# Cross-attention and soft mixture of experts on one core: second group's keys made early, norm factors folded, exponentials with sums

## The chip, the cores and the metric

The kernel runs on one core of a Trainium2 chip, in 32-bit floats throughout. The metric is device time in microseconds (us). The core has TensorE (PE), VectorE (DVE), ScalarE (ACT), GpSimd (POOL) and SyncE (SP), each with its own instruction queue that it works through in order; SP issues most of the DMAs.

## What is computed

For each of 16 batches, 100 tokens of width 256 attend to 361 context rows with 16 heads of width 16. The result goes through a soft mixture of 16 experts with 64 slots each.

```python
x = x + xattn(layernorm(x), ctx, ctx, mask, wq, bq, ..., wo, bo)   # 16 heads of 16
y = layernorm(layernorm(x)) * norm_g + norm_b
se = (layernorm(slot_embeds) * slot_g + slot_b) * scale            # 16 experts x 64 slots
logits = einsum("bnd,esd->bnes", y, se)
dispatch = softmax(logits, over the tokens n)
combine = softmax(logits, over all slots e, s)
slots = einsum("bnd,bnes->besd", y, dispatch)
h = gelu(slots @ Wg + bg) * (slots @ Wu + bu)                      # 256 -> 512
eout = h @ Wd + bd                                                 # 512 -> 256
out = x + einsum("bns,bso->bno", combine, eout)
```

## The kernel before

**Groups and stages.** The batches are worked in five groups of 2, 2, 4, 4 and 4 (line 47). For each group the attention makes the tokens' new x, then the dispatch of its logits fills slots, then 16 experts run over all slots of the group, and then the weighted sum goes to the output. The experts' weights are read again for each group, by SP's queue, into five buffers (`load_weights`, line 949).

**Attention.** `query_work` (403) normalises two batches' x, transposes it and makes queries. `key_work` (467) loads and transposes one batch's context and makes keys `kT` and values `vpad`; a row of the mask is put into `kT` by DMA (523). Keys of a batch take one of the two "kl" buffers, which the combine logits `lex` use too, so `keys_fit` (697) lets a group's keys begin only when few are held and, once one is held, when the dispatch of the groups before is done. A batch is then four units (`Unit`, 618): scores (634), maxima on VectorE (639), a transpose of the maxima (647) and their addition to the queries (649), scores again, transposed (657), exponentials on ScalarE (665), the product with the values (678). The sums come out of the same product as a further row. `out_work` (553) divides by them after the fourth unit, in two halves of 200 columns (565 to 568), multiplies with `wo`, adds x and normalises twice over in one step (597). POOL, or VectorE in the first group, multiplies by `norm_g` and adds `norm_b` (600, 601).

**Dispatch.** `slot_work` (362) makes the normalised slot embeddings `seT` once. `dispatch_quarter` (762) does four experts of two batches: logits `lg` (777); maxima over the tokens on VectorE (787) and a copy to `lgs` on ScalarE (789), both from the same PSUM tile; subtraction on POOL (794), exponentials (808), sums and reciprocal on VectorE (819, 820), product on POOL (822); transposes of these weights, `d_t` (829), and the slots `sl` (839), which VectorE (850) and ScalarE (853) write to the ring. `lgs` is transposed too, `lex_t` (805), for the softmax over slots in `combine_weights` (860).

**Experts.** `experts` (1001) makes for each expert gate `gp` and up `up` (1020), gelu on ScalarE (1031), the product `hT` on VectorE (1036), and in `down` (969) the product `dn` (981). `combine_quarter` (910) adds up the outputs.

**The ring.** One SBUF tile of 10240 columns holds slots and expert outputs, a region for each quarter of a group (740). Group 0 uses columns 0 to 4095. At the start the first columns hold slot embeddings and mask.

**What sets the order.** The order on each engine is fixed when the kernel is built. Every piece of work is a generator (`Task`, 95) that yields the time at which its next step can run and how many PSUM banks it needs. The loop at line 1080 keeps a planned clock for each engine (`Clock`, 55), with a cost for each operation, and picks the first task that is ready; units and dispatch come before side work (`fill`), experts last. Four PSUM banks of one tag, `mm`, are shared by all products but the scores. While the experts have not begun and nothing is ready on PE, the loop puts in a product of the identity with itself, `warm` (1068, 1118). These fillers give PE something to do and are not used.

```python
            if not begun and now + 0.2 < ready[first] and ck.bank_ready(1) <= now and now > 8.0:
                warm_up()
                continue
```

Of the kernel before, what the change touches and what calls it, by code (L numbers as in the profile page):

```python
# [115 lines left out]
def xattn_ffn_kernel(  # L116
# [101 lines left out]
    NPAR = 4 + E * FC  # L218
    par1 = const.tile([NPAR, P], F32, name="par1")
    par2 = const.tile([E * FC, P], F32, name="par2")  # L220
    for i, v in enumerate((slot_g, slot_b)):
        nc.gpsimd.dma_start(par1[2 * i : 2 * i + 2, :], v.rearrange("(a p) -> a p", p=P))
    nc.gpsimd.dma_start(par1[4:NPAR, :], bg.rearrange("e (a p) -> (e a) p", p=P))
# [26 lines left out]
    vpads = []  # L250
    for i in range(2):
        vp = const.tile([P, 3, H * 32], F32, name=f"vpad{i}")
        vp = vp.rearrange("p c (x k w) -> p c x k w", k=4, w=HD)
        for c in range(3):
            nc.vector.memset(vp[:, c, :, 1:3, :], 0.0)
            nc.vector.memset(vp[:, c, :, 1:3, 0:1], 1.0)
        vpads.append(vp)
# [21 lines left out]
    sb_c = [sgb[:, i : i + 1] for i in (2, 3)]  # L279

# [31 lines left out]
    def parameter_work():  # L312
# [5 lines left out]
        load_bc("ng", norm_g)  # L318
        load_bc("nb", norm_b)
        for _ in range(3):  # L320
            load_weights(0)
        yield 22.0, 1
# [38 lines left out]

    def slot_work():
# [3 lines left out]
        for c in range(ES // P):  # L366
            yield (lambda: max(25.0, ck.t["DVE"])), 0
            t = ck.run("DVE", stats(se[:, c, :], P, mv[:, c, :]))
# [7 lines left out]
        for c in range(ES // P):  # L376
            yield (lambda: max(t, ck.t["ACT"])), 0
# [19 lines left out]
        seT_t[0] = last  # L397

    seT_t = [NEVER]
    with_bo = {}  # L400
    qps, keys, values_t, cxs_of, out_t = {}, {}, {}, {}, {}
# [65 lines left out]
    def key_work(b):  # L467
# [20 lines left out]
        kT = None  # L488
        for oc in range(KD):
            yield (lambda: max(t, par_t[0], 7.0) if kT or keys_fit(b) else NEVER), 1  # L490
            if not kT:
                live.add(b)
                kT = two.tile([P, KD, 2, S2], F32, tag="kl", name="kT")
# [34 lines left out]
        vp = vpads[b % 2]  # L528
# [24 lines left out]
    def out_work(b):  # L553
# [3 lines left out]
        cxs, t = cxs_of[b]  # L557
        comb = cxs[:, 0]
        yield t, 0
        rs = const.tile([P, 2, KD, N], F32, tag="rs", name="rs")  # L560
        t2 = t
        for par in range(2):
            if par:
                yield t, 0
            nc.vector.stream_shuffle(rs[:, par], cxs[:, par], [MAXROW[par]] * 32)
            nc.vector.reciprocal(rs[:, par], rs[:, par])
            t = ck.run("DVE", 1.65, t)
            nc.gpsimd.tensor_tensor(cxs[:, par], cxs[:, par], rs[:, par], ALU.mult)
            t2 = ck.run("POOL", 0.6, t)
        yield t2, 0  # L570
        nc.vector.tensor_tensor(comb, comb, cxs[:, 1], ALU.add)
        t = ck.run("DVE", 0.3, t2)
# [26 lines left out]
        engine = nc.gpsimd if g else nc.vector  # L599
        engine.tensor_tensor(z, z, bcs["ng"][:N], ALU.mult)  # L600
        engine.tensor_tensor(z, z, bcs["nb"][:N], ALU.add)
        t = ck.run("POOL" if g else "DVE", 1.45 if g else 0.7, t)
# [15 lines left out]
    class Unit:  # L618
# [11 lines left out]
        def maxima(self):  # L630
# [11 lines left out]
            self.t = ck.run("DVE", 1.66, ck.run("PE", 0.7, self.q_t, self.k_t, free_t[0]))  # L642
# [9 lines left out]
        def exponentials(self):  # L652
# [13 lines left out]
            self.t = free_t[0] = ck.act("exp", 1200, ck.run("PE", 0.7, self.t))  # L666
            if self.cb == 3:
                live.remove(self.b)

        def values(self):  # L670
            if self.cb == 0:
                live_cxs.add(self.b)
                cxs_of[self.b] = [two.tile([P, 2, KD, N], F32, tag="cxs", name="cxs"), 0.0]
            cx = mm_tile("cx")
            for c in range(3):
                n = KC if c < 2 else S2 - 2 * KC
                for r in range(4):
                    nc.tensor.matmul(  # L678
                        cx[32 * r : 32 * r + 32, :N],
                        lhsT=vpads[self.b % 2][  # L680
# [6 lines left out]
            nc.scalar.copy(cxs_of[self.b][0][:, self.par, self.oc, :], cx[:, :N])  # L687
            t = ck.copy(100, ck.run("PE", 0.55, self.t, values_t[self.b], ck.bank()))
            ck.free(t)
            cxs_of[self.b][1] = t  # L690

    free_t = [0.0]
    group_of = {b: g for g, n in enumerate(GROUPS) for b in range(starts[g], starts[g] + n)}
# [14 lines left out]
    def units(g):  # L708
        last = None

        def finish(u):
            u.values()
            if u.cb == 3:
                fill.append(Task(out_work(u.b), ck))
                if u.b + 1 in group and u.b + 2 in group:
                    fill.append(Task(key_work(u.b + 2), ck))
# [45 lines left out]
    def dispatch_quarter(g, p, q):  # L762
# [3 lines left out]
        def gate():  # L766
# [4 lines left out]
            return max(seT_t[0], out_t[starts[g] + b0 + 1])  # L771
# [13 lines left out]
        lgv = lg[:, : 4 * N].rearrange("p (c n) -> p c n", n=N)  # L785
        mx = two.tile([P, 4], F32, tag="mx", name="d_mx")
        nc.vector.tensor_reduce(mx, lgv, AX.X, ALU.max)  # L787
        lgs = two.tile([P, 4, N], F32, tag="lgs", name="lgs")
        nc.scalar.copy(lgs, lgv)  # L789
        tl = ck.copy(400, t)  # L790
        t = ck.psum_dve(400, t)
        ck.free(max(t, tl))
        ex = two.tile([P, 4, N], F32, tag="ex", name="d_ex")
        nc.gpsimd.tensor_tensor(ex, lgs, mx.unsqueeze(2).to_broadcast([P, 4, N]), ALU.subtract)  # L794
        t = ck.run("POOL", 0.95, t, tl)
        yield (lambda: max(t - 0.3, tl) if (g, p) in live or len(live) < 2 else NEVER), 1
# [11 lines left out]
        nc.scalar.activation(ex, ex, AF.Exp)  # L808
        t = ck.act("exp", 400, t)
# [7 lines left out]
        yield t, 0  # L817
        sm = two.tile([P, 4], F32, tag="sm", name="d_sm")
        nc.vector.tensor_reduce(sm, ex, AX.X, ALU.add)
        nc.vector.reciprocal(sm, sm)  # L820
        t = ck.run("DVE", 0.75, t)
        nc.gpsimd.tensor_tensor(ex, ex, sm.unsqueeze(2).to_broadcast([P, 4, N]), ALU.mult)
# [365 lines left out]
```

## Time and profile before

| | us |
|---|---|
| median of 3 runs | 1240.83 (1240.37 to 1244.67) |
| the profiled execution | 1242.1 |
| its span, first to last instruction | 1240.1 |
| mean granted TensorE clock | 0.994 of full |
| first expert product starts | 114.28 |
| PE without work until 20 us / 20 to 78 / 78 to 106 | 7.9 / 0.33 / 0.43 |

A line of a profile's timeline reads: start, duration, engine, source line, operation, output <- inputs, shapes, how many records; in brackets the idle time of the engine before it and what ended that. A 32-bit product is two records, a transpose one. "PEld" is the load of PE's stationary operand, which runs beside the products. A wait that names an engine is inferred from semaphores: it ended last there.

### The profile page before, as it was taken

Reading aid. Unit: us, or ns where it says so; the run is one execution under the profiler, and the core shown is the slowest. Engines: PE = TensorE matmul, PEld = TensorE weight load, DVE = VectorE, ACT = ScalarE, POOL = GpSimd, SP = SyncE. Lnnn points to the kernel's source line nnn. Section 1 sums busy time; section 2 is a strip of 40 time slices with the busy share of each in tenths; the row PEclk is TensorE's granted clock in tenths of the full one; section 3 lists DMA queues with packets and bytes.
Section 4 is the critical chain, followed back from the end, with each engine's and each line's share of the span. In section 5 each row is a group of like instructions: output and inputs, shape, how many; then the busy total and the mean of one; then the engine's idle time right before and its main releaser. Section 6 shows DMA issues by size and latency. Waiting matters only on the chain.

```text
span 1240.1 us, 23091 instructions
## 1 busy us (share of the span) xinstructions
PE 1213.2 (98%) x9545; PEld 1004.7 (81%) x9545; DVE 572.5 (46%) x1193; ACT 482.6 (39%) x844; POOL 126.8 (10%) x174
## 2 busy tenths in 40 slices
PE   7999999999999999999999999999999999999998
PEld 5887888887888887778777777878888888888887
DVE  4555654566455467644535446545322245322222
ACT  2425354554444454544453436434111164311111
POOL 2111010021011112101101001211000011000000
PEclk9999999999999999999999999999999999999999
DMA  7000577621766631144333321133454432445542
GB/s 215 23 15 2 160 205 215 201 89 53 221 215 199 204 105 38 33 137 122 98 115 103 111 74 40 58 114 119 128 160 154 128 94 86 132 145 156 159 140 78
DMA packets 109329, 150.11 MB, mean 121 GB/s; under 512 B 6257, under 2 KB 67881, under 8 KB 109225
## 3 DMA queue, kind: packets, MB, share of 16 engines
q1 hardware_dynamic: 108336, 146.84, 39.1%
q8 instruction: 76, 1.25, 0.4%
q0 software_dynamic: 608, 1.53, 0.4%
q10 hardware_dynamic: 280, 0.26, 0.1%
q14 instruction: 29, 0.23, 0.1%
HBM read 146.95 MB, written 1.66 MB: 120 GB/s over the span
## 4 chain that ended last, share of the span: by engine, by line
PE 91%; DVE 3%; DMA 3%; ACT 2%; issue 1%; SPq 0%; DVEq 0%; ACTq 0%
PE gp L1020 18%; PE dn L981 18%; PE up L1020 18%; PE po L919 5%; PE sl L839 4%; PE at L657 4%; PE at L634 4%; PE lg L777 4%; PE cx L678 3%; PE warm L1071 3%; PE k_ps L496 2%; PE v_ps L534 2%; PE o_ps L576 1%; PE c_t L886 1%; PE d_t L829 1%; PE lex_t L805 1%
## 5 line engine op out<-in xcount | busy, mean ns | idle before, releaser
L1020 PE MATMUL gp<-ring,wg 128*128 128x256 f32 (+1 forms) x1280 | 247.3, 340 | 0.9 <-DMA wg<-in_L_ffn_Wg_dram 0.9
L1020 PE MATMUL up<-ring,wu 128*128 128x256 f32 (+1 forms) x1280 | 246.1, 339 | 1.5 <-DMA wu<-in_L_ffn_Wu_dram 1.5
L1036 DVE SCALAR_TENSOR_TENSOR hT<-up,parT,ge 128x256 f32<-128x256 f32 (+1 forms) x320 | 120.0, 425 | 276.0 <-PE up L1020 197.0
L1031 ACT ACTIVATE ge<-gp,parT 128x256 f32<-128x256 f32 (+1 forms) x320 | 117.0, 429 | 323.0 <-PE gp L1020 312.6
L981 PE MATMUL dn<-wd,hT 128*128 128x256 f32 x1024 | 235.4, 380 | 0.0
L1020 PEld LDWEIGHTS gp<-ring,wg 128*128 128x128 f32 x1280 | 203.6, 191 | 26.1 <-issue 5.3
L1020 PEld LDWEIGHTS up<-ring,wu 128*128 128x128 f32 x1280 | 204.4, 191 | 23.4 <-DMA wu<-in_L_ffn_Wu_dram 1.7
L981 PEld LDWEIGHTS dn<-wd,hT 128*128 128x128 f32 x1024 | 190.7, 190 | 26.1 <-DVE d_mx L787 0.5
L639 DVE TENSOR_REDUCE mxp<-at 100x4 f32<-100x1444 f32 x64 | 106.2, 1660 | 52.2 <-PE at L634 51.9
L991 DVE TENSOR_TENSOR ring<-dn,bd_bc 128x512 f32<-128x512 f32 (+1 forms) x80 | 46.7, 584 | 132.8 <-PE dn L981 132.8
L665 ACT ACTIVATE aT<-at 121x1200 f32<-121x1200 f32 x64 | 75.0, 1171 | 55.7 <-PE at L657 41.5
L1031 ACT ACT_TABLE_LOAD x51 | 65.4, 1283 | 46.6 <-PE gp L1020 38.6
L839 PE MATMUL sl<-disp,xn 100*128 100x256 f32 x256 | 64.0, 394 | 5.2 <-DVE vpad L541 4.9
L665 ACT ACT_TABLE_LOAD x43 | 55.2, 1283 | 35.4 <-DVE q L649 20.9
L919 PE MATMUL po<-ring,combT 64*100 64x256 f32 x512 | 60.7, 383 | 0.0
L839 PEld LDWEIGHTS sl<-disp,xn 100*128 100x128 f32 x256 | 48.0, 194 | 14.8 <-DVE vpad L541 6.1
L634 PE MATMUL at<-kT,qp 32*100 32x361 f32 x512 | 55.7, 504 | 2.9 <-DMA kT<-mrow_d 2.9
L657 PEld LDWEIGHTS at<-q,kT 32*121 32x121 f32 x1536 | 46.4, 180 | 15.0 <-issue 9.9
L678 PEld LDWEIGHTS cx<-aT,vpad 120*32 120x32 f32 (+1 forms) x1536 | 32.2, 110 | 32.5 <-issue 23.9
L657 PE MATMUL at<-q,kT 32*121 32x100 f32 x1536 | 57.1, 277 | 0.0
L794 POOL TENSOR_TENSOR d_ex<-lgs,d_mx 128x400 f32<-128x400 f32 x32 | 27.3, 853 | 286.3 <-ACT lgs L789 284.0
L919 PEld LDWEIGHTS po<-ring,combT 64*100 64x100 f32 x512 | 41.7, 163 | 15.3 <-issue 4.9
(124 smaller groups left out, 1207.1 us busy)
## 6 DMA issues: line engine op xcount, KB each, us to landing
wg<-in_L_ffn_Wg_dram SPq DMA_DIRECT2D x80, 512.0 KB
wu<-in_L_ffn_Wu_dram SPq DMA_DIRECT2D x80, 512.0 KB
wd<-in_L_ffn_Wd_dram SPq DMA_DIRECT2D x80, 512.0 KB
bd_bc<-in_L_ffn_bd_dram SPq DMA_DIRECT2D x80, 128.0 KB
c_sb<-in_ctx_dram SPq DMA_DIRECT2D x16, 240.0 KB
c_sb<-in_ctx_dram SPq DMA_DIRECT2D x16, 121.0 KB
acc<-in_x_dram SPq DMA_DIRECT2D x8, 200.0 KB
out_dram<-acc SPq DMA_DIRECT2D x8, 200.0 KB
```

The lines of the kernel that those rows point to most:

```text
L634: nc.tensor.matmul(self.at[:N, r, :S2], lhsT=self.q[rows], rhs=self.k[rows], start=True, stop=True)
L639: nc.vector.tensor_reduce(mxv[:, :, m : m + 1], self.at[:N, :, :S2], AX.X, ALU.max, negate=True)
L657: nc.tensor.matmul(self.at[: KC + 1, r, c * N : (c + 1) * N], lhsT=self.k[rows, c * KC : c * KC + KC + 1], rhs=self.q2[rows], start=True, ...
L665: nc.scalar.activation(self.aT[: KC + 1], self.at[: KC + 1, :, : 3 * N], AF.Exp)
L678: nc.tensor.matmul(cx[32 * r : 32 * r + 32, :N], lhsT=vpads[self.b % 2][:n, c, 4 * self.oc + r, 2 * self.par : 2 * self.par + 2, :].rearra ...
L777: nc.tensor.matmul(lg[:, c * 2 * N : (c + 1) * 2 * N], lhsT=seT[:, kd, (2 * q + c) * P : (2 * q + c + 1) * P], rhs=xnTs[g][:, kd, b0 * N : ...
L839: nc.tensor.matmul(sl[:, kd * 256 : (kd + 1) * 256], lhsT=xns[g][:, b0 + i, kd * P : (kd + 1) * P], rhs=disp[:, i, :], start=True, stop=True,)
L919: nc.tensor.matmul(pos[i][:N, :D], lhsT=combs[g, p, q][rows, j, :], rhs=eouts_of(g, q)[rows, j, p, :], start=j == 0, stop=j == QE - 1,)
L981: nc.tensor.matmul(dn[:, i * D : (i + 1) * D], lhsT=hts[fc // FB][0].rearrange("p (f t) -> p f t", f=FB)[:, fc % FB, tt * P : (tt + 1) * P ...
L1020: nc.tensor.matmul(ps[:, f * T : (f + 1) * T], lhsT=weights[k][kind][:, kd, fc * P : (fc + 1) * P], rhs=slots_of(g, q)[:, j, kd].rearrange ...
L1031: nc.scalar.activation(ge[:, cols], ps[:, cols], AF.Gelu, bias=col(4, e, fc))
L1036: nc.vector.scalar_tensor_tensor(out=hT[:, cols], in0=ps[:, cols], scalar=col(NPAR, e, fc), in1=ge[:, cols], op0=ALU.add, op1=ALU.mult,)
```

## The change

- **Keys and values early.** Keys, values and value pads of batches 2 and 3 (group 1) get places of their own in the ring, behind group 0's regions. Group 1's x, queries and keys are made while group 0's units run, without `keys_fit`. Twelve clears prepare the new value pads.
- **Division per unit.** `out_work` starts with a batch's first unit and divides after each, in four pieces of 100 columns.
- **Norm folded.** `norm_g` and `norm_b` no longer touch the tokens. `seT` is multiplied by `norm_g` (on ScalarE), `norm_b` times `seT` becomes a column `cb` added to the logits, by 16 products of one column, and both are applied to the slots when they leave PSUM.
- **Exponentials with sums.** The subtraction on POOL and the sum on VectorE go; four exponentials of 100 columns take the maxima as bias and give sums. In group 0 they read the logits in PSUM, and VectorE makes `lgs`; in later groups ScalarE makes `lgs` first and the rest reads that. In group 0 the dispatch's product with the reciprocal is on VectorE.
- **Planner.** Planned PE costs of a unit's three products are raised (0.7, 0.7 and 0.55 to 0.87, 0.85 and 0.72). Before the experts begin, side work is held back while VectorE or ScalarE has a backlog. The reciprocal of the combine sums is put later.

```diff
-    NPAR = 4 + E * FC
+    NPAR = 8 + E * FC
...
-    for i, v in enumerate((slot_g, slot_b)):
+    for i, v in enumerate((slot_g, slot_b, norm_g, norm_b)):
...
+    early_kT, early_vpads = [], []
+    def early_work():
+        at = QE * NQ * GROUPS[0] * P
+        for i in range(2):
+            yield 16.0, 0
+            early_vpads.append(value_pads(ring[:, at : at + 3 * H * 32]))
+            ck.run("DVE", 1.1)
+            at += 3 * H * 32
+            n = KD * 2 * S2
+            early_kT.append(ring[:, at : at + n].rearrange("p (k t s) -> p k t s", k=KD, t=2))
+            at += n
...
-        load_bc("ng", norm_g)
-        load_bc("nb", norm_b)
+        yield 22.0, 1
         for _ in range(3):
             load_weights(0)
-        yield 22.0, 1
...
-        seT_t[0] = last
-    seT_t = [NEVER]
+        yield last, 1
+        ps = mm_tile("cb_ps")
+        for c in range(ES // P):
+            for kd in range(KD):
+                nc.tensor.matmul(
+                    ps[:, c : c + 1],
+                    lhsT=seT[:, kd, c * P : (c + 1) * P],
+                    rhs=nb_c[kd],
+                    start=kd == 0,
+                    stop=kd == KD - 1,
+                )
+        t = ck.run("PE", 3.5, last, ck.bank())
+        nc.vector.tensor_copy(cb, ps[:, : ES // P])
+        t = ck.run("DVE", 0.15, t)
+        ck.free(t)
+        for g in range(2):
+            for kd in range(KD):
+                yield t, 0
+                dst = seT[:, kd, g * 512 : (g + 1) * 512]
+                nc.scalar.activation(dst, dst, AF.Copy, scale=ng_c[kd])
+                last = ck.copy(512, t)
+            seT_t[g] = last
+    seT_t = [NEVER, NEVER]
...
+        early = group_of[b] == 1
+        kT = early_kT[b % 2] if early else None
         for oc in range(KD):
-            yield (lambda: max(t, par_t[0], 7.0) if kT or keys_fit(b) else NEVER), 1
-            if not kT:
+            yield (lambda: max(t, par_t[0], 7.0) if kT is not None or keys_fit(b) else NEVER), 1
+            if kT is None:
...
+        vp = values_of[b] = (early_vpads if early else vpads)[b % 2]
...
+        comb = None
+        for cb in range(4):
+            yield (lambda: cx_t.get((b, cb), NEVER)), 0
+            cxs = cxs_of[b]
+            oc, par = divmod(cb, 2)
+            mine, comb = cxs[:, par, oc], cxs[:, 0]
+            rs = const.tile([P, N], F32, tag="rs", name="rs", bufs=2)
+            nc.vector.stream_shuffle(rs, mine, [MAXROW[par]] * 32)
+            nc.vector.reciprocal(rs, rs)
+            t = ck.run("DVE", 1.05, cx_t[b, cb])
+            soon = b == GROUPS[0] - 1 and cb == 3
+            (nc.vector if soon else nc.gpsimd).tensor_tensor(mine, mine, rs, ALU.mult)
+            t = ck.run("DVE", 0.25) if soon else ck.run("POOL", 0.45, t)
             if par:
                 yield t, 0
-            nc.vector.stream_shuffle(rs[:, par], cxs[:, par], [MAXROW[par]] * 32)
-            nc.vector.reciprocal(rs[:, par], rs[:, par])
-            t = ck.run("DVE", 1.65, t)
-            nc.gpsimd.tensor_tensor(cxs[:, par], cxs[:, par], rs[:, par], ALU.mult)
-            t2 = ck.run("POOL", 0.6, t)
-        yield t2, 0
-        nc.vector.tensor_tensor(comb, comb, cxs[:, 1], ALU.add)
-        t = ck.run("DVE", 0.3, t2)
+                nc.vector.tensor_tensor(comb[:, oc], comb[:, oc], mine, ALU.add)
+                t = ck.run("DVE", 0.25, t)
...
-        engine = nc.gpsimd if g else nc.vector
-        engine.tensor_tensor(z, z, bcs["ng"][:N], ALU.mult)
-        engine.tensor_tensor(z, z, bcs["nb"][:N], ALU.add)
-        t = ck.run("POOL" if g else "DVE", 1.45 if g else 0.7, t)
...
-            self.t = ck.run("DVE", 1.66, ck.run("PE", 0.7, self.q_t, self.k_t, free_t[0]))
+            self.t = ck.run("DVE", 1.66, ck.run("PE", 0.87, self.q_t, self.k_t, free_t[0]))
...
-            return max(seT_t[0], out_t[starts[g] + b0 + 1])
+            return max(seT_t[q // 2], out_t[starts[g] + b0 + 1])
...
+        def copies(t):
+            for c in range(2):
+                part = slice(2 * c, 2 * c + 2)
+                nc.scalar.activation(
+                    lgs[:, part], lgv[:, part], AF.Identity, bias=cb[:, 2 * q + c : 2 * q + c + 1]
+                )
+                t = ck.copy(200, t)
+            return t
+        def maxima(src, t):
+            nc.vector.tensor_reduce(mx, src, AX.X, ALU.max, negate=True)
+            return ck.run("DVE", 0.6, t)
+        def exponentials(src, t):
+            for i in range(4):
+                nc.scalar.activation(
+                    ex[:, i],
+                    src[:, i],
+                    AF.Exp,
+                    bias=mx[:, i : i + 1],
+                    accum_out=sm[:, i : i + 1],
+                )
+                t = ck.act("exp", 130, t)
+            return t
+        if g:
+            tl = copies(t)
+            ck.free(tl)
+            t = maxima(lgs, tl)
+        else:
+            t = exponentials(lgv, maxima(lgv, t))
+            for c in range(2):
+                part = slice(2 * c, 2 * c + 2)
+                nc.vector.tensor_scalar_add(
+                    lgs[:, part], lgv[:, part], cb[:, 2 * q + c : 2 * q + c + 1]
+                )
+                tl = ck.psum_dve(200)
+            ck.free(max(t, tl))
+        yield t, 0
+        if g:
+            t = exponentials(lgs, t)
+            yield t, 0
...
+        nc.vector.reciprocal(sm, sm)
+        t = ck.run("DVE", 0.18, t)
+        late = nc.gpsimd if g else nc.vector
+        late.tensor_tensor(ex, ex, sm.unsqueeze(2).to_broadcast([P, 4, N]), ALU.mult)
+        t = ck.run("POOL", 0.95, t) if g else ck.run("DVE", 0.6)
...
+                for kd in range(KD):
+                    nc.tensor.matmul(
+                        sl[:, kd * 256 : (kd + 1) * 256],
+                        lhsT=xns[g][:, b0 + i, kd * P : (kd + 1) * P],
+                        rhs=disp[:, i, :],
+                        start=True,
+                        stop=True,
+                    )
+                t2 = ck.pe(512, td, ck.bank())
+                for kd in range(KD):
+                    dst = slots_of(g, q)[:, :, kd, b0 + i, :]
+                    srcv = sl[:, kd * 256 : (kd + 1) * 256].rearrange("p (e s) -> p e s", s=S)
+                    if i == 0:
+                        nc.vector.tensor_scalar(dst, srcv, ng_c[kd], nb_c[kd], ALU.mult, ALU.add)
+                        t2 = ck.psum_dve(256, t2)
+                    else:
+                        nc.scalar.activation(
+                            dst, srcv, AF.Identity, bias=nb_c[kd], scale=ng_c[kd]
+                        )
+                        t2 = ck.copy(256, t2)
...
+        if not g:
+            yield t, 1
+            yield from dispatch()
...
-        nc.scalar.activation(ex, ex, AF.Exp)
-        t = ck.act("exp", 400, t)
...
-        nc.vector.tensor_reduce(sm, ex, AX.X, ALU.add)
-        nc.vector.reciprocal(sm, sm)
-        t = ck.run("DVE", 0.75, t)
-        nc.gpsimd.tensor_tensor(ex, ex, sm.unsqueeze(2).to_broadcast([P, 4, N]), ALU.mult)
-        t = ck.run("POOL", 0.95, t)
...
-        nc.vector.reciprocal(sm, sm)
-        ck.run("DVE", 0.15, t2[-1])
         for q in range(NQ):
             yield t2[-1], 1
+            if q == 0:
+                nc.vector.reciprocal(sm, sm)
+                ck.run("DVE", 0.15, t2[-1])
...
-                if group:
+                if group > 1:
                     fill.append(Task(query_work(b0), ck))
                     fill.append(Task(key_work(b0), ck))
-                fill.append(Task(key_work(b0 + 1), ck))
-                if group == 0:
+                    fill.append(Task(key_work(b0 + 1), ck))
+                elif group == 0:
+                    fill.append(Task(key_work(1), ck))
                     fill.append(Task(parameter_work(), ck))
+                    fill.append(Task(early_work(), ck))
                     fill.append(Task(slot_work(), ck))
+                    load_x(1)
+                    fill.append(Task(query_work(2), ck))
+                    fill.append(Task(key_work(2), ck))
+                    fill.append(Task(key_work(3), ck))
...
+        if not begun:
+            urgent = ("units", "out_work", "dispatch_quarter") if group < 2 else ("out_work", "dispatch_quarter")
+            soonest = min((r for t, r in zip(tasks, ready) if t.kind in urgent), default=NEVER)
+            backlog = max(ck.t["DVE"], ck.t["ACT"]) - now
+            for i, t in enumerate(tasks):
+                if t.kind in urgent or group == 0:
+                    continue
+                ready[i] = max(ready[i], now + backlog - (1.8 if t.banks else 0.6))
+                slack = {"units": 1.6}.get(t.kind, 0.6)
+                if group > 1 and now < soonest < now + slack:
+                    ready[i] = max(ready[i], soonest + 0.01)
```

## The prediction

> **What bounds the kernel now.** I read the page first (engines, then the chain), then the timeline of the first units, of the first dispatch, and the busy time by stage.
>
> ```profile
> PE 1213.2 (98%) x9545; PEld 1004.7 (81%) x9545; DVE 572.5 (46%) x1193; ACT 482.6 (39%) x844; POOL 126.8 (10%) x174
> PE 91%; DVE 3%; DMA 3%; ACT 2%; issue 1%; SPq 0%; DVEq 0%; ACTq 0%
> L1071 PE MATMUL warm<-ident 128*128 128x128 f32 x274 | 38.4, 288 | 0.0
> ```
>
> PE works from end to end and is 91% of the chain, so the time is the sum of three things: the matmuls, the gaps between them, and the filler products (`warm`) that stand where PE would wait before the first expert. A wait on another engine counts only where PE has nothing queued in front of it. The table of matmuls in the built programs is the same before and after but for the filler, 137 products before and 114 after, and 16 tiny ones. So the sum can only move through filler, those 16, and PE's idle time. Its idle time now is 26.9 us: 8.7 before 106 us (nearly all first loads), 13.8 after it, 4.4 at the end.
>
> The next view is the timeline of one unit of the first group (start, duration, engine, line):
>
> ```profile
> 39.17 1.66 DVE L639 TENSOR_REDUCE mxp<-at 100x4 f32<-100x1444 f32 x1 [1.71 <-PE at L634]
> 39.69 1.60 PE L1071 MATMUL warm<-ident 128*128 128x128 f32 x12
> 41.13 0.25 PE L647 MATMUL at<-ident,mxp 100*128 100x100 f32 x1
> 41.42 0.26 DVE L649 TENSOR_TENSOR q<-at,qp 128x100 f32<-128x100 f32 x1
> 42.00 0.89 PE L657 MATMUL at<-q,kT 32*121 32x100 f32 x24
> 42.83 1.83 PE L1071 MATMUL warm<-ident 128*128 128x128 f32 x14
> 43.01 1.17 ACT L665 ACTIVATE aT<-at 121x1200 f32<-121x1200 f32 x1 [2.94 <-DVE rstd L357]
> 44.58 0.87 PE L634 MATMUL at<-kT,qp 32*100 32x361 f32 x8
> ```
>
> A unit takes 6.34 us (38.24 to 44.58): PE's own 2.3 us, the rest filler, 0.25 us a product (14 records, 7 products, from 42.83 to 44.58). The maxima end at 40.83, the transpose starts at 41.13; the exponentials end at 44.18, the next unit at 44.58: filler outlasts the wait by 0.3 to 0.4 us.
>
> The third view is the first dispatch, where VectorE's maxima and ScalarE's copy read the same PSUM tile:
>
> ```profile
> 96.90 0.56 DVE L787 TENSOR_REDUCE d_mx<-lg 128x4 f32<-128x400 f32 x1
> 97.50 0.49 ACT L789 COPY lgs<-lg 128x400 f32<-128x400 f32 x1 [2.77 <-DVE d_mx L787]
> 98.20 0.57 DVE L787 TENSOR_REDUCE d_mx<-lg 128x4 f32<-128x400 f32 x1 [0.73 <-PE lg L777]
> 98.81 0.49 ACT L789 COPY lgs<-lg 128x400 f32<-128x400 f32 x1 [0.81 <-DVE d_mx L787]
> ```
>
> The copy starts 0.04 us after the maxima end, both times: two readers of one tile take turns, though the planner lets them run together.
>
> **Filler and early keys.** Keys, values and queries of the second group move into the first group's units. That would replace filler, but the units get longer. VectorE now has in front of the query sum (L649 before) a shuffle and a reciprocal of half the width (halves of 374 and 1403 ns, about 0.94 us), and twelve clears of value pads (six each of 272 and 72 ns, 2.06 us). In the built order the later units hold up to 20 fillers where they held 16. Net: 23 fewer, 23 x 0.25 = **-5.75**. With no filler at all it would be -34, so that is the bound on this idea.
>
> **Norm folded in.** The scale and bias of the norm leave 14 pairs on POOL (20.3 us) and two on VectorE, all off PE's path: 0. They come back as 16 products of one column (`cb`). Bounds: a pass costs 0.035 us (24 of L657 in 0.83) to 0.125 (the filler, same weights); two passes each, 1.1 to 4.0. The filler has the same weight load but streams 128 columns, so I stay near it at 0.10 a pass, **+3.3**. Two 1 KB loads are added on POOL's queue (0.5 us each, ahead of its first power at 8.35, which has 1.8 us to spare) and two of 128 KB are dropped; SP's queue gets x and eight mask rows earlier, with expert weights queued behind, needed first at about 111: 0.
>
> **Waits in the first units.** I walked the built order by the rows' durations. ScalarE gets eight slot normalisations and one eviction ahead of a unit's exponentials (8 x 0.51 + 0.78), PE waits about 0.85; `cb` waits for three more evictions (0.75); VectorE's slot step waits for a 1.68 us POOL power ahead of maxima (0.45 and 0.15); the query evictions, alternating between VectorE and ScalarE (2.1 us, 81.44 to 83.55), push a query sum (0.5); two of 0.15 and 0.25. Sum 3.1, against 0.8 now: **+2.3**, between 0 (filler already covers) and 4.
>
> **The first dispatch.** For group 0 the new code exponentiates straight from PSUM on ScalarE, four rows with sums, and VectorE then reads the same tile for `lgs`. In the built program VectorE's `lgs` waits for the fourth exponential, and the second quarter's maxima stand behind it on VectorE, the second exponentials behind those. One exponential with its sum: 0.35 us (the 128x128 gelu with bias, 368 ns, less 28 columns; the read of the sum hides behind the next, as L875's 1.14 us period shows), four 1.45. From the end of the first `lg`: maxima 0.7, exponentials to 2.2, two `lgs` of 0.478 to 3.15, maxima 3.7, exponentials 5.2, `lgs` 6.15, a value eviction 6.5, reciprocal and product 7.25. PE has only 1.36 + 0.5 + 1.72 + 0.5 = 4.08 us of work there, so it waits **3.3**. The second pair of quarters repeats it without the value eviction, with a weight product and a unit's scores as cover: 2.35 and 0.25. Together **+5.9** (0 if the tile were free to both, 7.5 at 0.45 an exponential). [...]
>
> The stall of the old second group's keys goes:
>
> ```profile
> 124.70 1.13 PE L839 MATMUL sl<-disp,xn 100*128 100x256 f32 x4 [1.55 <-DVE vpad L541]
> 124.00:128.00 4.00, 3.30 (x20) 2.96 (x21) 2.62 (x7) 2.68 (x7) 0.85 (x1) 0.83 0.19 26
> 128.00:132.00 4.00, 4.00 (x43) 2.69 (x42) 1.73 (x3) 0.67 (x2) 0.00 (x0) 0.75 0.80 275
> ```
>
> (The last two lines are stretches: length, busy time of PE, PEld, DVE, ACT and POOL with counts, granted clock, DMA share, GB/s.) That is **-1.55**, and the clock granted in the 8 us after it (0.83, 0.75) lost 4 x 0.17 + 4 x 0.25 = 1.7: **-1.7**. [...] I take 1.5 for each of the two: **+3.0** (0 to 3.4).
>
> **Later groups.** ScalarE gains about 1.84 us a quarter: exponentials 1.45 for 0.54, two copies with bias 0.95 for 0.49, two slot evictions about 1.05 for 0.59. In the 86 us from 427 it is busy 46.3; with eight quarters, 61. It stays below PE. The chain from logits to dispatch weights comes to 4.5 us after as it does now without queueing, because POOL's subtraction (0.85) and VectorE's sum (0.56) go. Smaller reciprocals block VectorE for 0.94 in place of 1.78, and the combine reciprocal no longer holds it (11.4 us in 8 waits, none of which PE felt). Bounds -6 (half of the 13.8 of idle) to +8; I take 0.
>
> **Sum.** -5.75 + 3.3 + 2.3 + 5.9 - 1.55 - 1.7 + 3.0 = +5.5. Span 1240.1 + 5.5 = 1245.6, about 1247.6 as profiled (2.0 around the span); the median of the runs lies 1.3 under the profiled 1242.1, so 1246.3; I write **1246.5**.
>
> **Rivals.**
> - *ScalarE becomes the limit in the later dispatches* (chance 0.2). Six more table loads (1.28 each) and 1.84 us a quarter: if each of 28 quarters delays PE by 0.4 us, +11 us: 1258, slower. From 0.02 us a quarter up it decides the sign. For it: ten of some 25 quarters leave under 1.2 us between weights and PE's transposes. Against: ScalarE is 54% busy there.
> - *The dispatch stall is covered* (0.15). Then 5.9 and 3.0 drop out: 1237.5, no change. Against it stands the wait in the built order.
> - *Less blocking pays* (0.15). The 11.3 us of idle left after the first dispatch, and 3.4 of lost clock at 286 and 811, fall away: 1246.5 - 14.7 = 1232, faster. For it: four of those gaps wait for VectorE evictions. Against: they come where PSUM tiles turn over, which the change leaves.
> - *The change does not fill*: that is the forecast itself (0.5, own range 1240 to 1253): the filler is still 114.
>
> What a measurement of this kernel can tell from no change is about 0.5%: 1234.6 to 1247.0. The likeliest case straddles its upper edge (0.27 within, 0.23 slower); with 0.2 slower, and 0.15 and 0.15 split 0.13 to 0.02, that gives slower 0.43, same 0.42, faster 0.15. Range 1234 to 1259.
>
> **What would show it.** Right: filler about 28 us; two waits of PE at the dispatch transposes, of about 3.3 and 2.5 us, with VectorE's `lgs` waiting for ScalarE's exponentials; the granted clock below 1 after them; experts starting at about 114. Wrong: no such waits; the sixteen one-column products well off 3.3; PE's idle after 140 us away from 11 by over 6.

## The result, and the profile after

The changed kernel takes 1244.86 us (median of 13 runs, 1238.62 to 1250.62), the kernel before 1240.37 us beside it (13 runs, 1237.55 to 1245.42). The ratio is 1.003, with a 95% interval of 1.001 to 1.0051: some 4 us slower, inside the 0.5% that was to count as no change. The profiled execution took 1247.61 us with a span of 1245.5 us. That this span lies 0.1 us from the prediction's sum of 1245.6 is chance, since the runs of one kernel spread over 12 us.

First the page of the changed kernel, engines and chain:

```profile
PE 1215.5 (98%) x9531; PEld 1007.6 (81%) x9531; DVE 577.7 (46%) x1327; ACT 539.8 (43%) x1134; POOL 81.8 (7%) x141
PE 89%; ACT 5%; DVE 3%; DMA 2%; issue 1%; ACTq 0%; SPq 0%; DVEq 0%
```

POOL lost 45 us of work, ScalarE gained 57, and PE still carries the chain. Next the groups of matmuls (busy us, mean ns | idle ahead of them and who ended it) that answer to the prediction's terms:

```profile
L1156 PE MATMUL warm<-ident 128*128 128x128 f32 x228 | 33.9, 293 | 0.1
L884 PE MATMUL d_t<-ident,d_ex 128*100 128x128 f32 x128 | 18.9, 277 | 4.5 <-DVE d_ex L876 2.4 <-DVE d_sm L873 2.0
L422 PE MATMUL cb_ps<-parT,seT 128*128 128x1 f32 x32 | 5.0, 292 | 0.0
```

The 114 filler products are busy for 33.9 us, not the 28 that 0.25 each would give. Little of that is the clock: in run 5 below, where no low clock is recorded before 762 us, 114 are busy for 32.2 us. Busy time says too much here, because the records of products overlap: in the timeline below two filler products (97.70) last 0.61 us, but the next product starts 0.44 us after them. The dispatch transposes have the two waits that were foretold. The timeline of the first dispatch shows how they come about:

```profile
96.55 0.57 DVE L841 TENSOR_REDUCE d_mx<-lg 128x4 f32<-128x400 f32 x1 [1.70 <-PE lg L817]
97.16 0.34 ACT L846 ACTIVATE d_ex<-lg,d_mx 128x100 f32<-128x100 f32 x1 [2.32 <-DVE d_mx L841]
...
97.70 0.61 PE L1156 MATMUL warm<-ident 128*128 128x128 f32 x4
98.14 1.99 PE L577 MATMUL v_ps<-wv,cT 128*121 128x256 f32 x8
...
98.60 0.76 DVE L864 TENSOR_SCALAR lgs<-lg,cb 128x200 f32<-128x200 f32 x2 [1.48 <-ACT d_ex L846]
99.27 0.57 DVE L841 TENSOR_REDUCE d_mx<-lg 128x4 f32<-128x400 f32 x1
...
101.32 0.76 DVE L864 TENSOR_SCALAR lgs<-lg,cb 128x200 f32<-128x200 f32 x2 [1.48 <-ACT d_ex L846]
...
103.25 0.62 PE L884 MATMUL d_t<-ident,d_ex 128*100 128x128 f32 x4 [2.35 <-DVE d_ex L876]
...
117.19 1.31 PE L884 MATMUL d_t<-ident,d_ex 128*100 128x128 f32 x8 [2.02 <-DVE d_sm L873]
```

VectorE's `lgs` waits 1.48 us for the fourth exponential, the second quarter's maxima stand behind it, and the same turn is taken once more; PE then waits 2.35 us, and 2.02 us at the second pair of quarters (117.19). The stretches of 4 us (length, busy PE, PEld, DVE, ACT, POOL, granted clock, DMA share, GB/s) hold the surprise:

```profile
54.00:58.00 4.00, 4.00 (x23) 4.00 (x22) 0.61 (x4) 0.00 (x0) 0.00 (x0) 0.54 0.01 4
58.00:62.00 4.00, 4.00 (x38) 3.55 (x38) 1.04 (x2) 1.78 (x2) 0.39 (x1) 0.60 0.00 0
...
100.00:104.00 4.00, 1.59 (x12) 1.24 (x11) 2.62 (x8) 1.39 (x9) 0.00 (x0) 1.00 0.00 0
104.00:108.00 4.00, 4.00 (x26) 3.62 (x26) 1.81 (x4) 2.09 (x4) 0.00 (x0) 1.00 0.01 2
```

Behind the first wait the clock stays at 1.00. It falls between 54 and 62 us instead, where PE is busy all the time, with the one-column products (`cb`):

```profile
52.18 5.04 PE L422 MATMUL cb_ps<-parT,seT 128*128 128x1 f32 x32
...
58.32 1.55 PE L697 MATMUL at<-q,kT 32*121 32x100 f32 x24
```

The 24 records of score products at 58.32 take 1.55 us; in an undisturbed unit they take 0.89 (at 40.32).

**How the runs are compared from here on.** The times of one kernel scatter by up to 12 us and follow the granted clock: of the changed kernel's 13 runs the shortest took 1238.62 us at 0.998, the longest 1250.62 at 0.989. So each run's lost clock, (1 - granted clock) x span, is taken as a number of its own, and the rest of its time, called the *clean time*, stands beside it. Over 80 runs of the kernel before, on three chips (1234.6 on each), the clean time is 1234.6 us with a deviation of 1.0; over 13 of the changed one 1237.7 with 0.9. Both columns are means; a last digit of the clock is 1.2 us, so single runs are not read this way. Each ratio is taken against runs of the kernel before made beside that row's.

| kernel | median us | ratio to before, 95% | clean time | lost clock | runs |
|---|---|---|---|---|---|
| before | 1240.5 | | 1234.6 | 6.0 | 80 |
| changed | 1244.9 | 1.001 to 1.0051 | 1237.7 | 6.9 | 13 |
| 1 cb with 64 columns | 1242.5 | 1.001 to 1.0029 | 1238.0 | 4.6 | 22 |
| 2 no cb products | 1240.2 | 0.9983 to 1.0005 | 1235.2 | 4.6 | 13 |
| 3 lgs first | 1240.7 | 0.9979 to 1.0008 | 1234.1 | 5.7 | 13 |
| 4 keys not early | 1249.3 | 1.005 to 1.0084 | 1241.5 | 6.7 | 5 |
| 5 norm at xn eviction, lgs first | 1234.3 | 0.9912 to 0.9954 | 1230.4 | 3.5 | 6 |
| 6 one exponential in later groups | 1244.0 | 1.0002 to 1.0045 | 1236.2 | 7.6 | 14 |
| 7 cb products twice | 1252.4 | 1.0058 to 1.0099 | 1240.9 | 10.8 | 6 |
| 8 as 5, replanned | 1237.3 | 0.9953 to 0.9976 | 1234.7 | 2.9 | 13 |
| 9 as 5, less filler | 1233.4 | 0.9929 to 0.9955 | 1228.4 | 4.4 | 5 |
| 10 as 5, no filler | 1247.5 | 1.0035 to 1.0069 | (1219.7) | 26.8 | 6 |
| 11 as 9, one exponential | 1234.9 | 0.9942 to 0.9968 | 1227.3 | 6.4 | 5 |

Run 10's clean time is in brackets: its clock is also low while PE only waits (from 40 to 41 us PE is busy for 0.05 us, at a clock of 0.50), where there is nothing to slow down, so the correction takes off too much.

### The profile page after: what moved, and what is told of

The parts are those of the page before. It is cut to its first block, busy times and chain, and to the rows that moved or that the text cites. A ratio compares the mean times of both kernels' runs of the same rounds, so it can differ in the third digit from the quotient of the medians.

```text
span 1245.5 us, 23498 instructions
## 1 busy us (share of the span) xinstructions
PE 1215.5 (98%) x9531; PEld 1007.6 (81%) x9531; DVE 577.7 (46%) x1327; ACT 539.8 (43%) x1134; POOL 81.8 (7%) x141
## 4 chain that ended last, share of the span: by engine, by line
PE 89%; ACT 5%; DVE 3%; DMA 2%; issue 1%; ACTq 0%; SPq 0%; DVEq 0%
PE dn L1066 18%; PE gp L1105 17%; PE up L1105 17%; PE po L1004 4%; PE at L697 4%; PE sl L894 4%; PE at L674 4%; PE lg L817 3%; PE k_ps L539 3%; PE v_ps L577 3%; PE cx L719 3%; PE warm L1156 2%; DMA wg<-in_L_ffn_Wg_dram 2%; ACT d_ex L846 1%; PE o_ps L620 1%; PE d_t L884 1%
## 5 line engine op out<-in xcount | busy, mean ns | idle before, releaser
L611 POOL TENSOR_TENSOR cxs<-cxs,rs 128x100 f32<-128x100 f32 x63 | 25.1, 398 | 512.6 <-DVE rs L608 431.1
L697 PEld LDWEIGHTS at<-q,kT 32*121 32x121 f32 x1344 | 41.8, 185 | 14.7 <-issue 7.3
L728 ACT COPY cxs<-cx 128x100 f32<-128x100 f32 x64 | 15.6, 244 | 84.6 <-PE cx L719 84.2
L697 PE MATMUL at<-q,kT 32*121 32x100 f32 x1344 | 51.3, 283 | 0.6 <-DVE q L689 0.6
L719 PEld LDWEIGHTS cx<-aT,vpad 120*32 120x32 f32 (+1 forms) x1344 | 28.2, 110 | 28.6 <-issue 20.8
```

The source lines that it names most:

```text
L697: nc.tensor.matmul(self.at[: KC + 1, r, c * N : (c + 1) * N], lhsT=self.k[rows, c * KC : c * KC + KC + 1], rhs=self.q2[rows], start=True, ...
L719: nc.tensor.matmul(cx[32 * r : 32 * r + 32, :N], lhsT=values_of[self.b][:n, c, 4 * self.oc + r, 2 * self.par : 2 * self.par + 2, :].rearra ...
```

## The experiments

Two theories were open. One: the change gives back by `cb` and by the turn-taking what early keys earn. The rival: ScalarE, with 57 us more work, slows the later groups, and the first 120 us hardly matter.

**1. One-column products, widened.** Sixteen products of 64 equal columns in place of one column.

```diff
-    ps[:, c : c + 1], ... rhs=nb_c[kd],
+    ps[:, 64 * c : 64 * c + 64], ... rhs=nb_c[kd].to_broadcast([P, 64]),
```

> The sixteen products that make cb get 64 equal columns each in place of one; the order of all engines is as in the changed kernel, and so is the output. Theory A (products of one column look idle to the clock, so they were mis-sized and lower the clock behind them): the granted clock stays at 1.00 between 50 and 62 us, the 32 passes take about 4.0 us (0.125 each, as the filler's) in place of 5.0, the transpose behind them about 0.25 in place of 0.41, the scores behind that 0.89 in place of 1.55; 2 to 3 us less in all, about 1242. Rival B (the clock falls for another reason, for instance the 0.39 us wait ahead of them): the clock falls to 0.54 to 0.60 again, and the time stays at 1245 or grows.

The timeline and the stretches of this run:

```profile
51.55 3.79 PE L422 MATMUL cb_ps<-parT,seT 128*128 128x64 f32 x32
```

```profile
54.00:58.00 4.00, 4.00 (x52) 3.78 (x52) 1.58 (x6) 1.17 (x2) 0.40 (x1) 1.00 0.00 0
58.00:62.00 4.00, 4.00 (x52) 2.86 (x51) 2.60 (x4) 2.20 (x6) 0.00 (x0) 1.00 0.00 0
```

Sixty-four times the columns take 3.79 us where one column took 5.04, and the clock stays at 1.00. In run 3, where the low clock came only behind them, the one-column products took 3.73:

```profile
52.81 3.73 PE L422 MATMUL cb_ps<-parT,seT 128*128 128x1 f32 x32
```

So with the clock at 1.00, as it is from 52.81 to 56.54 us in run 3, one column takes what 64 take (3.73 and 3.79 us), and the difference is the clock. The clean time is the same within 0.3, the lost clock falls by 2.3, give or take 2: theory A.

**2. No such products.** `cb` is set to zero.

> Leaves the sixteen cb products out and sets cb to zero, so norm_b is missing from the logits; every other instruction stands in the same order. Theory A (cb stands on the path of a unit and costs its own 5.0 us less what the maxima cover, and the lost clock): maxima end 1.15 us after cb began, so PE waits about 1.2 us there and gains 3.8, and 1.7 us of slow products behind go as well: 5 to 5.5 us less, about 1239.5. Rival B (filler or a later wait takes the place, since exponentials and slot evictions on ScalarE set the pace): under 2 us less, 1243 to 1245.

```diff
-    ps = mm_tile("cb_ps")
-    for c in range(ES // P):
-        for kd in range(KD):
-            nc.tensor.matmul(ps[:, c : c + 1], ... rhs=nb_c[kd], ...)
...
-    nc.vector.tensor_copy(cb, ps[:, : ES // P])
+    nc.vector.memset(cb, 0.0)
```

In the timeline PE now waits for the maxima where `cb` stood (they end at 52.38; the profile names the clear of `cb` right behind them):

```profile
50.72 1.66 DVE L669 TENSOR_REDUCE mxp<-at 100x4 f32<-100x1444 f32 x1 [2.82 <-PE at L664]
52.43 0.30 PE L677 MATMUL at<-ident,mxp 100*128 100x100 f32 x1 [1.13 <-DVE cb L420]
```

Clean time 2.5 less than the changed kernel, lost clock 2.3 less: 4.8 us, a little under the 5 to 5.5 expected: theory A. The products' 3.7 us at full clock less the 1.13 that PE now waits are 2.6, near the clean time's 2.5.

**7. The products twice.** This run gives the dose.

```diff
-    for c in range(ES // P):
+    for c in list(range(ES // P)) * 2:
```

> The sixteen one-column products are made twice over, 64 passes in place of 32; output and all other orders are as in the changed kernel. Theory A (one-column passes cost 0.11 to 0.125 each on PE and lower the granted clock): 3.6 to 4.0 us more with the lost clock taken out (1241.5), and one or two more drops of the clock of 1.7 us each, 1247 to 1249 in all. Rival B (the lost clock behind cb was chance): 3.6 to 4.0 us more with the lost clock taken out, and the lost clock stays at about 6.9 us on average, 1248.5 at most with no drop of the clock between 52 and 66 us.

```profile
54.00:58.00 4.00, 4.00 (x27) 4.00 (x26) 0.00 (x0) 0.00 (x0) 0.00 (x0) 0.67 0.02 4
58.00:62.00 4.00, 4.00 (x21) 4.00 (x20) 0.00 (x0) 0.00 (x0) 0.00 (x0) 0.50 0.00 0
62.00:66.00 4.00, 4.00 (x37) 3.60 (x36) 1.66 (x6) 0.00 (x0) 0.40 (x1) 0.50 0.00 0
```

32 more passes add 3.2 us of clean time, 0.10 a pass, and the lost clock goes from 6.9 to 10.8, so that the low clock lasts from 55 to 69 us in the profile: theory A. The 1252.4 us lie over the 1247 to 1249 expected, because that figure was added up wrongly: 1241.5 of clean time, the 6.9 us already lost and one or two steps of 1.7 give 1250.1 to 1251.8. The five profiles with one-column products (changed, 3, 4, 6 and, twice over, 7) lose 3.41, 1.71, 3.41, 5.12 and 6.82 us of clock there; the six with 64 columns or no such products, and with filler (1, 2, 5, 8, 9, 11), lose nothing there.

**3. `lgs` before the exponentials.** In the first group only:

```diff
-    t = exponentials(lgv, maxima(lgv, t))
     for c in range(2):
         nc.vector.tensor_scalar_add(lgs[:, part], lgv[:, part], cb[...])
+    t = exponentials(lgs, maxima(lgs, t))
```

> In the first group VectorE writes lgs from PSUM first, then takes the maxima from lgs, and ScalarE exponentiates from lgs, so the two engines no longer take turns on one tile; PE's order is the same. Theory A (turn-taking made the two waits of 2.35 and 2.02 us at the dispatch transposes): from the end of the first logits lgs 0.8, maxima 0.57, exponentials 1.35, reciprocal and product 0.75, 3.6 us in all against the 7.2 seen; both waits fall under 0.5 us, about 4 us less, 1241. Rival B (something else is late next there, the value evictions or the second quarter's exponentials): at least one wait stays over 1 us and less than 2 us is gained, 1243 to 1245. Rival C (the waits stood in front of weights that were not there yet): the first wait for the weight transfer gets as much longer, 1245.

```profile
95.56 0.76 DVE L863 TENSOR_SCALAR lgs<-lg,cb 128x200 f32<-128x200 f32 x2 [1.70 <-PE lg L817]
96.36 0.57 DVE L841 TENSOR_REDUCE d_mx<-lgs 128x4 f32<-128x400 f32 x1
96.92 0.76 DVE L863 TENSOR_SCALAR lgs<-lg,cb 128x200 f32<-128x200 f32 x2
...
100.94 0.61 PE L885 MATMUL d_t<-ident,d_ex 128*100 128x128 f32 x4 [0.17 <-DVE d_ex L877]
```

VectorE goes through both quarters without a wait for ScalarE; PE's waits at these transposes sum to 0.7 us, against 4.5. Clean time 3.6 less. Theory A; the weights for the first expert were there in time.

**4. Keys not early.**

```diff
-    early = group_of[b] == 1
+    early = False
...
-    if group > 1:
+    if group:
...
-    fill.append(Task(early_work(), ck))
...
-    load_x(1)
-    fill.append(Task(query_work(2), ck))
-    fill.append(Task(key_work(2), ck))
-    fill.append(Task(key_work(3), ck))
```

> The changed kernel with keys, values and queries of the second group made after the first group's units, as in the kernel before; all other parts of the change stay. 138 filler products in place of 114. Theory A (early keys pay by the filler that they replace, 24 x 0.25 = 6 us, and by the stall and lost clock at the old place): 6 to 9 us slower, 1251 to 1254. Rival B (early keys only swap filler for longer units and pay nothing): within 2 us of the changed kernel, 1243 to 1247.

```profile
100.86 0.61 PE L884 MATMUL d_t<-ident,d_ex 128*100 128x128 f32 x4 [2.37 <-DVE d_ex L876]
```

Clean time 3.8 more, lost clock equal. Early keys pay, but less than theory A's 6 to 9: 24 fillers saved come to 0.16 us each. Part of their worth goes into the first group's longer units: with early keys the first dispatch transpose starts at 103.25, without them at 100.86, at equal lost clock. The old key stall doesn't come back in this order, so this run doesn't price it.

**6. One exponential in the later groups.**

```diff
+    nc.gpsimd.tensor_tensor(ex, lgs, mx.unsqueeze(2)..., ALU.add)
-    t = exponentials(lgs, t)
+    nc.scalar.activation(ex, ex, AF.Exp)
+    nc.vector.tensor_reduce(sm, ex, AX.X, ALU.add)
```

> In the groups after the first the dispatch weights are made as in the kernel before: POOL subtracts the maxima, ScalarE takes one exponential of 400 columns, VectorE sums; everything else, and PE's order, as in the changed kernel. Theory A (ScalarE stays below PE in the later dispatches, so its four exponentials with sums cost nothing): within 1 us of the changed kernel with the lost clock taken out (1237.7). Rival B (ScalarE is the limit there, and the later waits for gelus on ScalarE come from the exponentials): 3 us or more faster, 1234.7 or less with the lost clock taken out, and the waits for ge of 1.53, 1.34 and 1.30 us are gone. Rival C (the chain from logits to weights is longer in the old way, by the subtraction and the sum): 2 us or more slower.

Neither end: clean time 1.5 less. The groups show which waits go; in the changed kernel the same line has 2.6 us of idle ahead of it, for ScalarE's gelus (`ge`):

```profile
L1070 PE MATMUL dn<-wd,hT 128*128 128x256 f32 x1024 | 235.9, 381 | 0.0
```

The waits of 1.34 and 1.30 us at about 1000 us are gone; the one of 1.53 us near 773 stays, so not every wait for `ge` comes from the exponentials. Over 28 quarters, 1.5 us is 0.05 us each. In median time the two kernels can't be told apart (1244.0 and 1244.9).

**5. Both repairs.** The norm's scale and bias move to the eviction of the transposed `xn`, which makes `cb` and the four scalings of the embeddings needless; `lgs` goes first.

```diff
-    nc.scalar.copy(xnTs[g][...], ps[...])
+    for kd in range(KD):
+        nc.scalar.activation(xnTs[g][:, kd, ...], ps[...], AF.Identity, bias=nb_c[kd], scale=ng_c[kd])
```

> Two repairs together: norm_g and norm_b are applied where ScalarE evicts the transposed xn (two evictions of 100 columns in place of one of 200), so cb, its products and the four scalings of the embeddings go; and in the first group lgs is written before the exponentials. PE's order is otherwise that of the changed kernel. Theory A (the two costs are separate and add up): about 6 us less than the changed kernel once the lost clock is taken out (2.5 for cb, 3.6 for the turn-taking: 1237.7 to 1231.6) and about 2 to 3 us less lost clock, so 1236 to 1237 in all, which is 3 to 4 us under the kernel before. Rival B (one of them only uncovers the other): 4 us or less in all, 1240 to 1241, no better than the kernel before.

The two costs add up: clean time 7.3 less than the changed kernel where 6.1 was the sum of runs 2 and 3, lost clock 3.4 less. At 1234.3 us it is faster than both kernels, by 0.5 to 0.9% against the kernel before.

**8 to 11. What filler costs.** Run 8 drops `cb` from the planner's costs too, and the planner then puts 132 fillers; run 9 raises the smallest wait that is filled from 0.2 to 0.45 us (87 fillers); run 10 fills nothing; run 11 is run 9 with run 6's edit.

```diff
-    if not begun and now + 0.2 < ready[first] ...
+    if not begun and now + 0.45 < ready[first] ...   (run 10: if False)
```

> As the run with norm at the xn eviction and lgs first, but the order is planned anew without cb, which lets the planner put 132 filler products where the changed kernel has 114. Theory A (filler stands only where PE would wait, so more of it costs little): within 2 us of that run. Rival B (the planner overestimates the waits and each filler is paid, 18 x 0.25): about 4.5 us slower than that run, with the lost clock taken out.

Clean time 4.3 more than run 5, rival B: 18 x 0.24. In this order the value products that stood ahead of the first dispatch transpose (run 5, first line) have gone elsewhere, and filler stands there for them (run 8, second line):

```profile
92.22 1.89 PE L563 MATMUL v_ps<-wv,cT 128*121 128x256 f32 x8
95.98 2.39 PE L1140 MATMUL warm<-ident 128*128 128x128 f32 x20
```

> The run with norm at the xn eviction and lgs first, and filler only where the planner sees a wait of over 0.45 us in place of 0.2: 87 filler products for 114. Theory A (the last filler before each step outlasts the wait, so every product saved counts about 0.24): 27 x 0.24 = 6.5 us less than that run with the lost clock taken out (1230.4 to 1224), lost clock unchanged at 3 to 4 us, about 1228 in all. Rival B (at the margin the filler only fills real waits): within 1 us of that run. Rival C (the short gaps that are left lower the clock): 2 us or more of lost clock on top.

A miss for theory A: 27 fillers fewer gave 2.0 us of clean time, 0.07 each, not 0.24. So most of the time of these last fillers was waiting that remains without them. In median time, runs 5 and 9 can't be told apart (1234.3 and 1233.4).

> The same run with no filler at all: PE waits where filler stood. Theory A (filler is needed for the clock, and half of it outlasts the waits): with the lost clock taken out some 7 to 12 us less than with 114 products, and 10 us or more of additional lost clock in the first 110 us, so no faster in all, 1234 to 1245. Rival B (waits between units are too short to lower the clock): lost clock unchanged, 1224 to 1228 in all.

The stretch that covers most of the first group's units, granted clock third from the right:

```profile
40.00:80.00 40.00, 31.84 (x332) 20.59 (x332) 21.02 (x50) 16.16 (x28) 4.93 (x8) 0.69 0.04 11
```

Waits of 0.4 to 1.6 us in the units suffice to keep the clock down, at 0.69 over these 40 us: 26.8 us are lost on average, and the run takes 1247.5 us, over the 1234 to 1245 expected and 13 us over run 5, which fills with 114 products and loses 3.5. This kernel needs filler for the clock.

> The run with 87 filler products, and in the groups after the first one exponential of 400 columns with POOL's subtraction and VectorE's sum, as in the kernel before. Theory A (what the exponentials with sums cost ScalarE in the later groups adds up with the rest): 1.5 us less than with 87 products alone, with the lost clock taken out, and the two waits for ge of 1.3 us gone. Rival B (those 1.5 us were chance): the same time within 0.5 us.

The two waits for `ge` at about 1000 us are gone again and the clean time is 1.1 less than run 9's, but in median time the two can't be told apart (1234.9 and 1233.4), so the gain isn't settled.

## Why the prediction was right, and where its terms were not

The total came out right, with terms that missed in both directions. The parts measured on their own in clean time are early keys -3.8 (run 4), `cb` +2.5 (run 2), turn-taking +3.6 (run 3), the later exponentials +1.5 (run 6): +3.8, against 1237.7 - 1234.6 = +3.1 for the whole change. The sum of parts is good to about 2 us only, since the changed kernel's mean enters it four times. About 1 us of lost clock comes on top, and that figure is no surer than the scatter of 13 runs (2.5 to 13.7 each). The prediction's own terms come to +4.2 of clean time and +1.3 of lost clock. That the dispatch, 2.3 too dear, and the later exponentials, put at nothing, largely made up for each other is luck. Whether the kernel would come out slower or unchanged the prediction left open, with chances of 0.43 and 0.42.

- *Filler, -5.75, and waits in the first units, +2.3.* The count of filler was right (114). The two terms share one stretch of time, and both were too large. The trace has two waits in the changed units, 0.39 us at 50.73 and 0.59 at 74.94, 1.0 in all where 3.1 was foretold; for that a filler was worth some 0.17 us, not 0.25. Together -3.45 was foretold, and run 4 has -3.8: the misses cancel.
- *`cb`, +3.3.* The price of a pass was about right: 0.10 foretold, 0.10 by run 7's clean time, 0.12 in run 3's timeline (3.73 for 32). That the products lower the clock was not seen: they cost 2.5 clean and some 2.3 of lost clock. Of all terms this is the one whose mechanism was incomplete.
- *The dispatch, +5.9.* The mechanism was right, step by step, down to the wait for the fourth exponential. The size was 4.4 in the trace, 3.6 by run 3. (By its own steps the first wait is 7.25 - 4.08 = 3.2, where it writes 3.3.) Mis-sized were the exponential with its sum (a period of 0.32 us in the timeline, 0.35 assumed), `lgs` (0.76 for two, 0.96 assumed), and the second pair, where PE felt one wait of 2.02.
- *The old key stall, -1.55.* It is gone: behind 117.19 PE next waits until 143.97, for 0.40 us. What that is worth no run shows.
- *Clock behind the two stalls, +3.0, and -1.7 at the old place.* No run shows the 1.5 us that was taken for each of the two waits at the dispatch transposes. None was lost at them in the profiled run. Over the profiles that have these waits, the first (2.36 us) lost 1.7 in four of six and the second (2.03 us) in two of five, 1.8 together on average. The prediction took as a fixed price what depends on where the wait falls in time (last section).
- *Later groups, 0.* Idle after 140 us is 13.1 us, within the foretold range of 11 give or take 6; the exponentials cost 1.5. ScalarE's load came out as worked out (60.7 us of the 86 from 427, for 61), which is 71%; the 54% that the prediction set against the rival was that of the kernel before. The rival with 0.4 us a quarter is excluded, by run 6's 0.05. The rival that the stall is covered is excluded by the two waits, the one of less blocking by the idle time.

## What to carry to other kernels

A scale or bias that is moved to save work on an idle engine must land where the data passes anyway: here two evictions with scale and bias in place of a plain one cost nothing that shows (run 5), sixteen small products cost 4.8 us (run 2). Count two readers of one PSUM tile as one queue, and copy the tile out first: in the first dispatch of the kernel before, ScalarE's copy started 0.04 us after VectorE's maxima had ended; in the changed kernel VectorE's `lgs` started 0.04 us after ScalarE had its last sum (98.56); with the copy first, PE's waits there fell from 4.5 to 0.7 us (run 3). Compare kernels on one core with the lost clock taken out; 0.3% that drowns in the scatter is then plain to see.

## What the runs showed of the hardware

**One-column products act on the clock as a wait does.** PE is busy for 4.00 of 4 us with one column as with 64; with one the granted clock is 0.50 to 0.67 over 4 us (changed kernel, run 7), with 64 it is 1.00 (run 1).

**Lost clock comes in equal steps on a fixed grid.** Summed over stretches of 1 us, every drop behind a wait or behind these products costs 1.7 us or a multiple (1.71, 3.41, 5.12, 6.82). The clock records in the traces show the grid: within one execution the drops start whole multiples of 3.413 us apart (in the changed kernel at 54.36, 774.57 and 1030.57, 211 and then 75 of them), and each lasts one, two or more of them at half clock. At half clock one stretch of 3.413 us loses 1.7, which is the step. These stretches of the grid are called windows below. What sets the grid no run shows.

**A wait counts by what falls into one window.** The first dispatch wait shows it. In the changed kernel the end of a window cuts it in two, and the clock stays; in run 6 the same wait lies within one window, and the next window has half the clock. The stretches are windows of the grid, laid out from the starts of the drops, two of the changed kernel, then two of run 6. Length less busy PE is the idle time, 1.30 and 1.11 us in the changed kernel against 2.41 in run 6:

```profile
98.73:102.14 3.41, 2.11 (x11) 1.54 (x9) 1.93 (x6) 1.41 (x8) 0.00 (x0) 1.00 0.04 14
102.14:105.56 3.42, 2.31 (x18) 2.27 (x19) 1.92 (x6) 1.14 (x2) 0.00 (x0) 1.00 0.00 0
...
100.81:104.23 3.42, 1.01 (x8) 0.65 (x7) 2.14 (x7) 1.22 (x8) 0.00 (x0) 1.00 0.00 0
104.23:107.64 3.41, 3.41 (x17) 3.21 (x16) 0.60 (x2) 1.17 (x2) 0.00 (x0) 0.50 0.00 0
```

Over all profiles that have one or both of the two dispatch waits, six windows with 2.10 us or more of idle were followed by half the clock, and none with 1.79 or less. A wait of 1.53 us in all twelve profiles of the changed kernel and its variants shows the same. Five lose 3.41 us behind it, seven nothing: in the five it lies within one window, in the seven the end of a window cuts it, and no window has more than 1.28 us of idle. The changed kernel is one of the five:

```profile
773.50 1.13 PE L894 MATMUL sl<-disp,xn 100*128 100x256 f32 x4 [1.53 <-ACT ge L1116]
```

```profile
771.16:774.57 3.41, 1.88 (x11) 1.12 (x9) 1.50 (x4) 3.36 (x9) 0.00 (x0) 1.00 0.00 0
774.57:777.98 3.41, 3.41 (x30) 2.77 (x30) 1.07 (x3) 2.40 (x2) 0.00 (x0) 0.50 0.00 0
```

The one-column products fit in: each first drop there follows a window with 1.75 us or more of them, and 0.8 us in a window (run 3) did not suffice. Where the grid lies differs from execution to execution: in the profiles of the changed kernel and of runs 3, 6 and 7 the first drop starts at 54.36, 57.04, 53.02 and 55.34 us, which divided by 3.413 leaves 3.16, 2.43, 1.82 and 0.73. So before a run the loss is a matter of chance. No single figure of idle fits all places (near 1020 us 1.2 us in a window sufficed in three profiles), and what decides between one step and two these runs don't show.
